# Column transform over 128 rows by moving turned chunks on chip, with fixed engine order and an earlier spectrum of the next image

## Chip, cores and metric

The kernel runs on one core of one Trainium2 chip. The metric is the device time of one execution in microseconds (us), the median of several runs. "PE" is TensorE, "DVE" VectorE, "ACT" ScalarE, "POOL" GpSimd and "SP" SyncE, which here does nothing but issue transfers.

## The reference, cut to what matters

The input is eight images of 8 channels, 256 by 256, in float32. After a group norm, four Fourier layers follow, then a two-layer head per pixel, and at the end a 3 by 3 dilation of the normed result.

```python
for i in range(4):
    h1 = _spectral_conv(h, sp_w1[i], sp_w2[i])   # rfft2, keep 12x12 low modes, mix channels, irfft2
    h2 = _gconv1x1(h, w_w[i], w_b[i])
    h = h1 + h2
    if i < 3:
        h = _gswish(h, betas[i])
h = _gswish(_gconv1x1(h, fc1_w, fc1_b), betas[3])   # head: 10 -> 128 per group
return _gconv1x1(h, fc2_w, fc2_b)                   #       128 -> 2 per group
```

The kernel does the transforms as matmuls with small cosine and sine tables. The *column transform* is the forward transform over the 256 columns (w), done for each chunk of 24 image rows as soon as the chunk has its new values. There are 11 chunks an image and layer, and layers 0, 1 and 2 need the column transform for the layer after them.

## The kernel before

PE is in program order (`manual_schedule(engines={PE})`); the other engines' order is left to the scheduler. A generator writes out the layers of image b and, after each `yield n`, some steps of the head of image b-1 (128 in all, in proportion to the counts n). `unit(main, late)` writes `main` now and the `late` part of the unit before it just after, so that a unit's dependent half comes one unit later.

```python
def turn(c):                                   # 32x32 blocks transposed by VectorE
    nc.vector.transpose(turned[:, c % 3], h[:, c].rearrange("p f w -> p (f w)"))
    ...                                        # returns the pair (c-1, c) when c is odd

def transform(chunks):                         # two chunks together, K = 32 rows
    ...
    for v in range(8):                         # 8 steps over the 256 columns
        for f in range(NQ):
            for q in range(NQ):
                mm(pair[q // 2][part(f), q % 2, :m], fw8[part(q), v, :],
                   t[part(q), :, f, :, v, : NBLK * WID], start=v == 0, stop=v == 7)
    ...                                        # copies to z, half on VectorE, half on ACT

def burst(c):                                  # a chunk of one layer
    ...                                        # 16 matmuls h2 (L461 or L458), 8 matmuls h1 (L464)
    nc.scalar.activation(dst, pair[i], AF.Silu)
    ...
    if l < 3:
        ready.append(turn(c))

for c in range(NCH):
    before = ready[c - 1] if l < 3 and c > 0 else None
    unit(partial(burst, c), partial(transform, before) if before is not None else None)
    yield 1
```

Between layers stand the row transform, the mixing by the spectral weights (`mix`, whose weights are loaded when they are needed) and the rebuilding of rows (`rows_of`); each has copies out of PSUM that alternate between VectorE and ACT. Each image begins with the spectrum of its own x.

Of the kernel before, what the change touches and what calls it, by code (L numbers as in the profile page):

```python
# [21 lines left out]
G = 4  # L22
# [17 lines left out]
STEPS = 128  # L40


@with_exitstack
def fno_dilate_kernel(ctx: ExitStack, tc: tile.TileContext, a: dict, out: bass.AP):
    nc = tc.nc
    mm = nc.tensor.matmul
    PE = mybir.EngineType.PE
# [25 lines left out]
    fw8 = load("fw8", (128, 8, 32))  # L73
# [8 lines left out]
    eh_q = load("eh_q", (128, 3, NBLK, 32))  # L82
# [7 lines left out]
    cz = load("cz", (32, 4, WID, G, 2))  # L90
# [9 lines left out]
    turned = const.tile([128, 3, 2048], F32, tag="turned", name="turned")  # L100
# [3 lines left out]
    for t in y_rows:  # L104
        for r in (0, C * HW + 1):
            nc.sync.dma_start(t[r : r + 1], yin[0:1, 0, :HW])
    fz = const.tile([128, WID, G, 32], F32, tag="fz", name="fz")
# [49 lines left out]
    for l in range(3):  # L157
        nc.vector.tensor_tensor(
            cz[0:1, l, :, :, 0], cz[0:1, l, :, :, 0],
            sp_a[0:1, 4 * l : 4 * l + 4].unsqueeze(1).to_broadcast([1, WID, G]), ALU.mult,  # L160
        )
    nc.vector.tensor_tensor(cz[0:1, 0, :, :, 0], cz[0:1, 0, :, :, 0], cv[0:1], ALU.add)
    nc.sync.dma_start(cz[25:26, 0, :, :, 0], cv[1:2])
    nc.sync.dma_start(cz[0:1, 0, :, :, 1], cv[2:3])
# [9 lines left out]
    def group_stats(chunks, name):  # L174
        n = len(chunks)
        st = sb.tile([128, n, 6], F32, tag="bn", name=f"bn_{name}")
        for i, c in enumerate(chunks):
            nc.vector.bn_stats(st[:, i, :], c)
        return stats_end(st, name)

    def stats_end(st, name):
        mv = sb.tile([128, 2], F32, tag="mv", name=f"mv_{name}")
        nc.vector.bn_aggr(mv, st.rearrange("p n s -> p (n s)"))
        p = ps_a(f"p_st_{name}")
        mm(p[:, 0:1], grp, mv[:, 0:1], start=True, stop=True)
        mr = sb.tile([128, 2], F32, tag="mr", bufs=4, name=f"mr_{name}")
        nc.vector.tensor_copy(mr[:, 0:1], p[:, 0:1])
        d = sb.tile([128, 1], F32, tag="d", name=f"d_{name}")
        nc.vector.tensor_tensor(d, mv[:, 0:1], mr[:, 0:1], ALU.subtract)
        nc.vector.scalar_tensor_tensor(mv[:, 1:2], d, d, mv[:, 1:2], ALU.mult, ALU.add)  # L190
        q = ps_a(f"p_sv_{name}")
        mm(q[:, 0:1], grp, mv[:, 1:2], start=True, stop=True)
        nc.vector.tensor_scalar(mr[:, 1:2], q[:, 0:1], EPS, None, ALU.add)
        nc.scalar.activation(mr[:, 1:2], mr[:, 1:2], AF.Sqrt)
        nc.vector.reciprocal(mr[:, 1:2], mr[:, 1:2])
        return mr
# [19 lines left out]
    def spectrum_x(b, out_):  # L216
# [6 lines left out]
        mr = group_stats([x[:, i // 4, 512 * (i % 4) : 512 * (i % 4 + 1)] for i in range(8)], f"x{b}")  # L223
        out_["mr"] = mr
        yield 1
        a0 = sb.tile([128, 128, 16], F32, tag="Z", bufs=1, name=f"a0_{b}")
        xt = turned[:, 2].rearrange("p (f r c) -> p f r c", f=2, r=8)
        for half in range(2):
            xn = x[:, half]
            nc.vector.tensor_scalar(xn, xn, mr[:, 0:1], mr[:, 1:2], ALU.subtract, ALU.mult)  # L230
            xn = xn.rearrange("p (r w) -> p r w", r=8)
            yield 1
            for r in range(0, 8, 4):
# [8 lines left out]
                nc.vector.tensor_copy(dst[:, 0], src[:, 0])  # L242
                nc.scalar.copy(dst[:, 1], src[:, 1])
# [11 lines left out]
        yield 1  # L255
# [39 lines left out]
    def spectrum_h(b, l, at, out_):  # L295

        rows = turned.rearrange("p t f -> p (t f)")[:, : NBLK * WID * 128]
        if l % 2 == 1:

            view = rows.rearrange("p (i g k) -> p i g k", g=G, k=32)  # L300
            for j0 in range(0, NBLK * WID, 8):
                n = min(8, NBLK * WID - j0)
                t = ps_z(f"p_at_{b}_{l}_{j0}")
                for i in range(n):
                    nc.tensor.transpose(
                        t[: CS * NQ, i // 4, 128 * (i % 4) : 128 * (i % 4 + 1)],
                        at[:, :CS, :, j0 + i].rearrange("p r j -> p (r j)"), ident)
                dst = rows[: CS * NQ, 128 * j0 : 128 * (j0 + n)]
                src = t[: CS * NQ].rearrange("p u w -> p (u w)")[:, : 128 * n]
                if (j0 // 8) % 2 == 0:  # L310
                    nc.vector.tensor_copy(dst, src)
                else:
                    nc.scalar.copy(dst, src)
                if j0 == 8:
                    yield 1
            eh, m = eh_f, CS * NQ
            yield 1
        else:

            view = rows.rearrange("p (g i k) -> p i g k", g=G, k=32)  # L320
            for g in range(G):
                nc.vector.transpose(
                    rows[:, 960 * g : 960 * (g + 1)].rearrange("p (i r) -> p i r", r=32),
                    at[:, :, g, : NBLK * WID].rearrange("p r i -> p i r"))
            eh, m = eh_q, 128
            yield 2
        p = ps_a(f"p_b_{b}_{l}")
        for k in range(2):
            for n in range(2 * NBLK):
                term, blk = n // NBLK, n % NBLK  # L330
                for q in range(4):
                    k0 = 12 * term + 3 * q
                    mm(p[part(q), 120 * k : 120 * k + 120], eh[:, spectrum_table(k, term), blk, :],
                       view[:m, WID * blk : WID * (blk + 1), :, k0 : k0 + 3],
# [13 lines left out]
    def mix(b, l, bt):  # L348

        s = [sb.tile([128, 3, G, 2, WID], F32, tag=f"S{i}", bufs=1, name=f"S{i}_{b}_{l}") for i in range(2)]  # L350
        for k in range(3):
            sw = sb.tile([128, G, 2 * WID, WID], F32, tag="sw", name=f"sw_{b}_{l}_{k}")
            nc.sync.dma_start(sw.rearrange("p g m i -> p (g m i)"), a["spw"][l, k])
            for k2 in range(2):
                pr = turned[:, 2, 1024 * k2 : 1024 * k2 + 800].rearrange("p (g m i) -> p g m i", g=G, i=WID)
                nc.vector.tensor_tensor(  # L356
                    pr, sw, bt[:, k2, k].unsqueeze(2).to_broadcast([128, G, 2 * WID, WID]), ALU.mult)
# [3 lines left out]
                )  # L361
        f = sb.tile([128, 2, 3, G, WID], F32, tag="F", bufs=1, name=f"F_{b}_{l}")
        nc.vector.tensor_tensor(f[:, 0], s[0][:, :, :, 0, :], s[1][:, :, :, 1, :], ALU.subtract)
        nc.vector.tensor_tensor(f[:, 1], s[0][:, :, :, 1, :], s[1][:, :, :, 0, :], ALU.add)
        yield 6
# [7 lines left out]
        nc.vector.tensor_copy(fz[0:32, :, :, 24:26], cz[:, l])  # L373
        for q in range(4):
            dst = fz[part(q), :, :, 6 * q : 6 * q + 6].rearrange("p o g k -> p k g o")
            src = p[part(q), :240].rearrange("p (k g o) -> p k g o", g=G, o=WID)
            if q % 2 == 0:
                nc.vector.tensor_copy(dst, src)
            else:
                nc.scalar.copy(dst, src)  # L380
        yield 1

    def rows_of(b, l, out_):

        z = sb.tile([128, 32, NQ, 32], F32, tag="Z", bufs=1, name=f"Z_{b}_{l}")
        nc.gpsimd.memset(z[:, :CS, :, NBLK * WID :], 0.0)
        nc.gpsimd.memset(z[:, CS:], 0.0)
        zv = z[:, :CS, :, : NBLK * WID].rearrange("p r f (n o) -> p o n r f", n=NBLK)
        for o in range(0, WID, 2):
# [10 lines left out]
            for u in range(2):  # L400
# [7 lines left out]
                if u == 0:  # L408
                    nc.vector.tensor_copy(dst, src)  # L409
                else:  # L410
                    nc.scalar.copy(dst, src)
            if o % 4 == 2:
                yield 1
        out_["z"] = z
        yield 1


    def layer(b, l, z, mr, stored):
        def turn(c):

            nc.vector.transpose(turned[:, c % 3], h[:, c].rearrange("p f w -> p (f w)"))  # L421
            if c % 2 == 1:
                return (c - 1, c)
            return (c,) if c == NCH - 1 else None

        def transform(chunks):

            done.append(chunks)
            order = sorted(chunks, key=lambda c: c % 3)
            n = len(order)  # L430
            lo = order[0] % 3
            step = order[-1] % 3 - lo if n == 2 else 1
            t = turned[:, lo : lo + step * (n - 1) + 1 : step].rearrange(
                "p n (f s v i) -> p n f s v i", f=NQ, s=2, v=8)
            m = 2 * n * NBLK * WID
            pair = [ps_z(f"p_d_{b}_{l}_{order[0]}_{i}") for i in range(2)]
            for v in range(8):
                for f in range(NQ):
                    for q in range(NQ):
                        mm(pair[q // 2][part(f), q % 2, :m], fw8[part(q), v, :],  # L440
                           t[part(q), :, f, :, v, : NBLK * WID], start=v == 0, stop=v == 7)
            for i in range(2):
                for k, c in enumerate(order):
                    dst = z[:, 2 * c : 2 * c + 2, 2 * i : 2 * i + 2, : NBLK * WID].rearrange("p s q i -> p q s i")
                    src = pair[i][:, :, 60 * k : 60 * k + 60].rearrange("p q (s i) -> p q s i", s=2)
                    if i == 0:
                        nc.vector.tensor_copy(dst, src)  # L447
                    else:
                        nc.scalar.copy(dst, src)  # L449
# [334 lines left out]
```

## Time and profile before

| | before |
|---|---|
| median of 4 fast runs (lowest, highest) | 5608.66 us (5593.67, 5617.1) |
| PE busy | 4647.9 us, 83% of the span |
| DVE, ACT busy | 2109.8 us (38%), 2860.7 us (51%) |
| bytes moved by DMA, packets | 354.52 MB, 74256 |
| mean granted clock of PE | 0.909 |

PE is the engine nearest to its limit, so what matters is which waits stand in front of PE's instructions. The view of waits has, for each engine and line, whom it waited for, the total in us, how many times, and the longest. These are four of the longest entries of PE:

```profile
PE p_d L440 <- issue: 215.4, 136, 4.3
PE p_g L393 <- ACT fz L380: 98.5, 16, 15.0
PE p_sv_x L192 <- DVE mv_x L190: 79.5, 8, 14.3
PE p_xt L236 <- ACT turned L243: 78.3, 13, 10.7
```

The second and the fourth say that PE stood still until ACT had finished a copy, the third that it stood for the statistics of x. They are what the smaller parts of the change go after. The forty slices, the groups and the timeline of this kernel are in the prediction.

### The profile page before, as it was taken

The page shows a single profiled execution, that of the slowest core. Times are in us where ns is not written, and L with a number is a line of the kernel's source. Part 1 is how long each engine was busy: PE and PEld are TensorE (multiplying, and loading weights), DVE is VectorE, ACT ScalarE, POOL GpSimd, SP SyncE. Part 2 cuts the span into 40 slices and gives each one's busy share as a digit, 9 for nine tenths or more (in the row PEclk, how much of TensorE's full clock was granted, in tenths as well). Part 3 has the DMA queues.
Part 4 walks back from the last instruction along what each step waited for, and adds up shares of the span by engine and source line. Part 5 has one row for each costly group of instructions (what it writes and reads, how often), then busy time and mean ns, then how long its engine had stood idle before and what let it go on. Part 6 is the DMA issues. An engine that isn't in the chain of part 4 may idle for free. (4 is left out here: it accounts for less than half of the span.)

```text
span 5622.9 us, 171099 instructions
## 1 busy us (share of the span) xinstructions
PE 4647.9 (83%) x80490; PEld 1907.3 (34%) x80490; DVE 2109.8 (38%) x2627; ACT 2860.7 (51%) x3269; POOL 280.2 (5%) x428
## 2 busy tenths in 40 slices
PE   5667899968998788887989779997799977999892
PEld 2433343323333233432434223342333423433220
DVE  5334333362333633245333442334433353332303
ACT  1223555545555445554555445554455544555682
POOL 1000000010000100000000000000000010000100
PEclk7779899979999799998999888998899988999996
DMA  2003100420014200041111411114101231102311
GB/s 62 11 11 143 36 34 30 148 81 23 32 41 156 69 34 29 26 162 64 34 41 47 141 56 37 34 60 140 50 30 34 97 118 36 34 30 102 101 61 49
DMA packets 74256, 354.52 MB, mean 63 GB/s; under 512 B 12691, under 2 KB 13967, under 8 KB 46863
## 3 DMA queue, kind: packets, MB, share of 16 engines
q0 software_dynamic: 37248, 176.18, 9.4%
q1 hardware_dynamic: 36303, 167.39, 8.7%
q8 instruction: 631, 10.34, 0.8%
q14 instruction: 74, 0.61, 0.0%
HBM read 217.70 MB, written 125.83 MB: 61 GB/s over the span
## 5 line engine op out<-in xcount | busy, mean ns | idle before, releaser
L529 ACT ACTIVATE act<-p_fc 128x1024 f32<-128x1024 f32 x2048 | 1981.7, 1022 | 627.1 <-PE p_fc L526 603.8
L526 PE MATMUL p_fc<-hs,c_w 32*128 32x512 f32 x8192 | 1458.8, 676 | 62.3 <-DVE o L584 29.1
L542 PE MATMUL p_fc<-act,c_w 128*32 128x512 f32 x8192 | 1177.0, 641 | 18.1 <-ACT act L529 13.5
L421 DVE STREAM_TRANSPOSE turned<-h 128x2048 f32<-128x2048 f32 x264 | 610.2, 2311 | 1082.2 <-ACT h L470 1082.2
L440 PE MATMUL p_d<-turned,c_fw 32*32 32x120 f32 (+1 forms) x36864 | 582.9, 275 | 346.5 <-issue 215.4
L470 ACT ACTIVATE h<-p_z 128x1024 f32<-128x1024 f32 x528 | 511.7, 1021 | 541.9 <-PE p_z L464 541.8
L526 PEld LDWEIGHTS p_fc<-hs,c_w 32*128 32x128 f32 x8192 | 485.0, 193 | 860.2 <-issue 360.4
L440 PEld LDWEIGHTS p_d<-turned,c_fw 32*32 32x32 f32 x36864 | 463.9, 106 | 539.8 <-issue 275.2
L461 PE MATMUL p_z<-h,c_wt 32*32 32x512 f32 x8448 | 517.3, 607 | 17.0 <-issue 9.4
L464 PE MATMUL p_z<-c_binv,Z 32*128 32x256 f32 x5632 | 439.6, 428 | 0.4 <-issue 0.4
L542 PEld LDWEIGHTS p_fc<-act,c_w 128*32 128x32 f32 x8192 | 167.9, 111 | 732.7 <-issue 672.8
L449 ACT COPY Z<-p_d 128x120 f32<-128x120 f32 x264 | 56.8, 263 | 681.6 <-PE p_d L440 681.6
L464 PEld LDWEIGHTS p_z<-c_binv,Z 32*128 32x128 f32 x5632 | 273.0, 197 | 323.9 <-issue 312.1
L447 DVE COPY Z<-p_d 128x120 f32<-128x120 f32 x264 | 63.5, 278 | 763.6 <-PE p_d L440 763.6
L472 DVE TENSOR_SCALAR h<-p_z,c_bias 128x1024 f32<-128x1024 f32 x88 | 112.9, 1283 | 359.5 <-PE p_z L464 359.5
L461 PEld LDWEIGHTS p_z<-h,c_wt 32*32 32x32 f32 x8448 | 96.2, 103 | 345.9 <-issue 107.9
L458 PE MATMUL p_z<-h,wc 6*32 6x512 f32 x2816 | 193.2, 668 | 8.2 <-issue 4.5
L409 DVE COPY Z<-p_g 128x264 f32<-128x264 f32 x160 | 98.0, 619 | 262.3 <-PE p_g L393 155.4
L393 PE MATMUL p_g<-c_rowg,fz 128*128 128x264 f32 x320 | 101.4, 466 | 98.5 <-ACT fz L380 98.5
L356 DVE TENSOR_TENSOR turned<-sw,B 128x800 f32<-128x800 f32 x192 | 180.5, 980 | 0.8 <-DMA sw<-in_spw 0.6
L358 DVE TENSOR_REDUCE S<-turned 128x80 f32<-128x800 f32 x192 | 179.4, 974 | 0.0
L546 DVE SCALAR_TENSOR_TENSOR y<-p_fc,c_b,y 128x512 f32<-128x512 f32 x64 | 47.9, 748 | 339.7 <-PE p_fc L542 339.7
(133 smaller groups left out, 2348.9 us busy)
## 6 DMA issues: line engine op xcount, KB each, us to landing
stored<-h SPq DMA_DIRECT2D x88, 1024.0 KB
hs<-stored POOLq DMA_DIRECT2D x88, 1024.0 KB, 5.1
sw<-in_spw SPq DMA_DIRECT2D x96, 400.0 KB
yin<-y_rows POOLq DMA_DIRECT2D x64, 512.0 KB, 4.8
h<-in_xp SPq DMA_DIRECT2D x352, 48.0 KB
turned<-in_x SPq DMA_DIRECT2D x16, 1024.0 KB
y<-in_x POOLq DMA_DIRECT2D x64, 256.0 KB, 3.0
y_rows<-y POOLq DMA_DIRECT2D x64, 256.0 KB, 2.3
```

Source lines behind the costliest of these rows:

```text
L356: nc.vector.tensor_tensor(pr, sw, bt[:, k2, k].unsqueeze(2).to_broadcast([128, G, 2 * WID, WID]), ALU.mult)
L358: nc.vector.tensor_reduce(s[k2][:, k].rearrange("p g s o -> p (g s o)"), pr.rearrange("p g m i -> p (g m) i"), AX.X, ALU.add,)
L421: nc.vector.transpose(turned[:, c % 3], h[:, c].rearrange("p f w -> p (f w)"))
L440: mm(pair[q // 2][part(f), q % 2, :m], fw8[part(q), v, :], t[part(q), :, f, :, v, : NBLK * WID], start=v == 0, stop=v == 7)
L458: mm(o, wc[k, :], h[k, c, f, :], start=True, stop=False)
L461: mm(o, wt[part(q), l, g, :], h[part(q), c, f, :], start=True, stop=False)
L464: mm(pair[q // 2][:, q % 2, HW * s : HW * (s + 1)], z[part(q), 2 * c + s].rearrange("p f o -> p (f o)"), binv[part(q), :], start=False, st ...
L470: nc.scalar.activation(dst, pair[i], AF.Silu)
L472: nc.vector.tensor_scalar(dst, pair[i], bias3, None, ALU.add)
L526: mm(pair[g // 2][:, g % 2, :], w1[part(g), blk, :], hs[c][part(g), j, :], start=True, stop=True)
L529: nc.scalar.activation(act[:, 2 * i : 2 * i + 2, :], pair[i], AF.Silu)
L542: mm(acc[part(g), :], w2[:, g, 15 - rb : 47 - rb], act[:, g, :], start=rb == 0, stop=rb == 15)
```

## The change

The intent has four parts. (1) The column transform shall contract 128 rows in two steps instead of 32 rows in eight; for that a turned chunk must lie the other way round over the partitions, so after the turn sixteen transfers move its blocks from one on-chip buffer to another. (2) VectorE and ACT get the program order too. (3) The spectrum of the next x and its first mixing stand beside the last layer of the image before. (4) The copies in the chains between layers go to VectorE, the weights of the mixing are loaded a layer earlier, and the chains get more places for head steps. A transform runs two chunks after its turn, which should hide the move.

```diff
-    with tc.manual_schedule(engines={PE}):
+    with tc.manual_schedule(engines={PE, DVE, ACT}):
...
-    turned = const.tile([128, 3, 2048], F32, tag="turned", name="turned")
+    turned = const.tile([128, 4, 2048], F32, tag="turned", name="turned")
...
         def turn(c):
+            k = c % 2
+            nc.vector.transpose(
+                turned[:, k].rearrange("p (v r i) -> p r v i", v=8, r=2 * NQ),
+                h[:, c].rearrange("p f (s v i) -> p (f s) v i", s=2, v=8))
+            src = turned[:, k].rearrange("p (v u x) -> p v u x", v=2, u=4)
+            dst = turned[:, 2 + k].rearrange("p (v q x) -> p v q x", v=2, q=NQ)
+            for q in range(NQ):
+                for u in range(4):
+                    nc.sync.dma_start(dst[part(u), :, q, :], src[part(q), :, u, :])
+
+        def transform(c):
+            t = turned[:, 2 + c % 2].rearrange("p (v q f s i) -> p v q f s i", v=2, q=NQ, f=NQ, s=2)
+            p = ps_a(f"p_d_{b}_{l}_{c}")
+            for v in range(2):
+                for g in range(G):
+                    m = t[:, v, g] if group_in_f else t[:, v, :, g]
+                    mm(p[part(g), :240], fw[:, v, :], m[:, :, :, : NBLK * WID], start=v == 0, stop=v == 1)
...
+        def after(c):
             if l < 3:
-                ready.append(turn(c))
+                turn(c)
+                if c > 1:
+                    transform(c - 2)
...
+            unit(partial(burst, c), partial(after, c))
+            next(side, None)          # a piece of the next x's spectrum, in layer 3
+            yield CHUNK               # CHUNK = 1.5
...                                   # zt replaces Z; fz, xt, at and row copies on VectorE;
...                                   # load_sw() a layer ahead; more yields in stats_end, mix, rows_of
```

## The prediction

> **What bounds the kernel now.** I read the forty slices first, then a table of three stretches, then the costliest groups, then two short pieces of the timeline. From the slices (busy tenths; PEclk is the granted TensorE clock):
>
> ```profile
> PE   5667899968998788887989779997799977999892
> PEclk7779899979999799998999888998899988999996
> DMA  2003100420014200041111411114101231102311
> ```
>
> TensorE is busy 80 to 90% of most slices, with seven dips. The first four slices are image 0, which has no head (fc1, silu, fc2) of an earlier image beside it; the dips that follow are the spectra of the next x. The table of stretches has length, then busy time of PE, weight loads, DVE, ACT, POOL, then granted clock, DMA share and GB/s:
>
> ```profile
> 216.00:254.00 38.00, 28.66 (x801) 14.91 (x792) 16.57 (x14) 15.24 (x19) 0.00 (x0) 0.90 0.01 3
> 511.00:5208.00 4697.00, 4041.68 (x70386) 1649.21 (x70388) 1776.03 (x2183) 2492.24 (x2849) 215.78 (x338) 0.93 0.19 63
> 5208.00:5623.00 415.00, 292.84 (x2086) 77.82 (x2080) 103.09 (x166) 256.13 (x265) 34.70 (x58) 0.86 0.21 69
> ```
>
> So the span is about 511 us for image 0, 4697/7 = 671 us for each of images 1 to 7, and 415 us of last head and dilation. In the middle PE is at 4042/4697 = 86% and the next engine, ACT, at 53%: PE's own stream of work sets the pace. The groups that the change touches:
>
> ```profile
> L440 PE MATMUL p_d<-turned,c_fw 32*32 32x120 f32 (+1 forms) x36864 | 582.9, 275 | 346.5 <-issue 215.4 <-ACT act L529 74.3 <-DVE turned L421 52.5
> L421 DVE STREAM_TRANSPOSE turned<-h 128x2048 f32<-128x2048 f32 x264 | 610.2, 2311 | 1082.2 <-ACT h L470 1082.2
> ```
>
> L440 is the column transform, 36864 small matmuls, 73 us of PE an image. The two pieces of timeline give the unit costs. First image 0 (start, length, engine, line, what, idle before it):
>
> ```profile
> 233.40 1.15 PE L464 MATMUL p_z<-c_binv,Z 32*128 32x256 f32 x16
> 234.58 1.94 ACT L470 ACTIVATE h<-p_z 128x1024 f32<-128x1024 f32 x2 [1.39 <-PE p_z L464]
> 236.55 2.31 DVE L421 STREAM_TRANSPOSE turned<-h 128x2048 f32<-128x2048 f32 x1 [1.01 <-ACT h L470]
> 238.92 4.55 PE L440 MATMUL p_d<-turned,c_fw 32*32 32x120 f32 x222 [4.37 <-DVE turned L421]
> ```
>
> This is the chain that decides my prediction: after a chunk's last matmul come two silus (1.94) and the turn (2.31), and PE, with nothing else to do, stood 4.37 us before the transform. Before the change that happens once for two chunks, in image 0 alone. With a head beside it:
>
> ```profile
> 818.86 1.07 PE L542 MATMUL p_fc<-act,c_w 128*32 128x512 f32 x8
> 819.85 1.16 PE L461 MATMUL p_z<-h,c_wt 32*32 32x512 f32 x32
> 820.94 1.15 PE L464 MATMUL p_z<-c_binv,Z 32*128 32x256 f32 x16
> ```
>
> A chunk's burst costs 2.2 us at full clock, one fc2 1.0, one fc1 about the same, so a head step 2.1.
>
> **What the skill says.** TensorE: Matmul & The Clock Gate, Part 1, says that PE runs at half clock after about 3.4 us of idleness and comes back after about as long busy. The trace agrees: in image 0, with its waits, slices are granted 0.7 to 0.9, in the middle mostly 0.9 and more. Part 3 of that page says that matmuls with 32 output columns overlap in different column groups; the trace has it in L542, eight instructions of about 640 ns each in 1.07 us. DMA: Bandwidth & Descriptors, Rules for kernel authors, says to coalesce many small transfers, as those under 64 KB pay mostly overhead. The trace shows the overhead as issue time on the SP queue, for loads on all partitions or on 32 (c_cz):
>
> ```profile
> 8.24 0.43 SPq L66 DMA_DIRECT2D c_wbd<-in_wbd  x1
> 8.72 0.43 SPq L66 DMA_DIRECT2D c_cz<-in_cz  x1
> 9.19 0.42 SPq L66 DMA_DIRECT2D c_wt<-in_wt  x1
> ```
>
> That is one per 0.47 us whatever the size. The landing record of a lone 1 KB transfer on this queue (issue at 21.96, landed at 23.24) adds about 1.2 us at the end.
>
> **The change part by part.**
>
> *Column transform.* 16 matmuls of 32 rows by 32 columns and 8 steps become 8 of 128 rows by 32 columns and 240 wide, 16 instructions a chunk. Counted by the L542 row, 16 x 240 = 3840 columns against 8 x 512 = 4096 in 1.07 us: 1.0 us a chunk instead of 73/33 = 2.2. Gain at most 33 x 1.2 = 40 us of PE an image, if it waits for nothing.
>
> *The move.* Each turn now ends with 16 transfers on SP of 64 KB, two runs of 1 KB on 32 partitions. Their bytes are little: a 1 KB packet takes 46 ns in the trace's packet records, 64 a DMA engine is 2.9 us. Their issue is not: 16 x 0.47 = 7.5 us for plain shapes. For two runs a partition I take 0.57 (my estimate: one third to one half of the 39% by which the POOL queue's two-level yin loads, 0.756 us, exceed its plain 0.545). So 16 x 0.57 + 1.2 = 10.3 us from the end of the turn to the last landing.
>
> *Is it hidden?* It looks as if two chunks hide it, since transform(c-2) follows turn(c). But turn(c) is called first, both use the buffer c mod 2, and the program order counts. In the built order the third turn's transfers (chunk 2) wait for no PE at all, and the first transform (chunk 0) waits on eight DMA semaphores for counts that only the transfers of chunk 2 reach. So the transform of c-2 reads what was just moved for c, and PE, which is in order, waits for the whole of turn(c): the intended lag is zero. (The values are then another chunk's rows. I put that error into a copy of the reference on the host and the output changed by 2e-6 at most, so it isn't caught by a comparison.) It holds for chunks 2 to 10 of three layers: 27 waits an image, 216 in all.
>
> *A waiting chunk.* From the end of the burst: 0.1 + 1.94 + 0.03 + 2.31 + 0.05 = 4.4, moves 10.3, transform 1.9 (half clock after such a wait), next burst 2.85 (the first half cold). That is 19.5 us. In the order of images 1 to 7, one fc2 and fc1 stand within the wait and cost nothing; 35 head steps of 128 fall into these 27 chunks, the 8 others stand outside: 8 x 2.3 / 27 = 0.7. So 20.2, and 27 x 20.2 = 545 us an image.
>
> *The rest of an image.* 93 head steps x 2.1 = 195; 17 chunks without the wait x 2.2 = 37; rows, inverse, mixing and x matmuls about 62 (by the rows of the costliest groups, a share of an eighth each, pipelined); 26 left for VectorE chains. 320 us. Here are the change's other parts: the x spectrum beside the last layer removes most of the dips, of which an image holds 671 x 14% = 94 us of idle PE; copies on VectorE instead of ACT cost nothing seen, as DVE is at 38%. I believe in a gain of some 30 to 50 us from these, and it is in the 320.
>
> *Image 0.* 85 us until the first burst as now, 27 x 19.5 = 527, 6 free chunks 20, transforms at the layer ends 9, three chains of about 40 us between layers (310 to 345 us is one now), 55 for the last layer, 50 for the rest of x and mixing beside nothing: about 870.
>
> *Sum.* 870 + 7 x (545 + 320) + 410 = 7335 us. I say 7350.
>
> **Rivals.** (1) The lag works as meant and the moves are hidden. The one-chunk delay of each transform call and the two extra buffers speak for it; the semaphore counts speak against. Then 671 - 40 - 45 = 586 an image, image 0 about 470, in all 470 + 7 x 586 + 410 = 4980, 11% faster. (2) The shape makes each issue dear: the only many-run SP transfer now, c_cz<-cv with 40 pieces, took 0.70 to 0.83 us. At 0.8 + 0.04 the moves take 14.6 instead of 10.3: 4.3 x 27 x 8 = 930 more, 8270. For it: that measurement; against: those are 4-byte pieces, and stored<-h with 128 pieces takes 0.35. (3) Moves issue at 0.38 (0.33 for a lone sw load, plus the gap): 7.3 us, 3 x 216 = 650 less, 6690. (4) VectorE becomes the bound through the fixed order: its 2110 us plus some 150 of copies is far below; I give it nothing.
>
> **Range and chances.** The issue interval, 0.38 to 0.84 us, spans 6690 to 8270 by itself and is what I know least; the clock after waits and the 320 add some 150 either way, partly cancelling. 6650 to 8250 holds 8 in 10. Even with moves of 7.3 us, a full clock and no leftover chain, an image needs 27 x 15.6 + 294 = 715 us, over the 671 of now, so the slower side has 0.95. I leave 0.03 for faster (the wait isn't what I read) and 0.02 for the same.
>
> **What would show it.** A p_d group of 4224 instructions with a long wait before it ended by DMA turned, some 12 us 216 times; SP busy with 4224 transfers at 0.4 to 0.6 us each in trains of sixteen; granted clock below 0.8 in the middle stretch; PE at some 55 to 65% of the span; image 0 near 870 us. Waits of p_d under 3 us, or a PE share above 85%, would prove the central step wrong. DMA intervals away from 0.57 would only shift the size.

## The result and the profile after

| | before | after |
|---|---|---|
| median of 4 fast runs | 5608.66 us | 8039.36 us |
| lowest to highest | 5593.67 to 5617.1 | 8034.96 to 8041.6 |
| ratio of fast runs | | 1.4337 (95% interval 1.43 to 1.4374) |
| PE busy | 4647.9 us (83%) | 4665.3 us (58%) |
| bytes by DMA, packets | 354.52 MB, 74256 | 627.58 MB, 411621 |
| mean granted clock | 0.909 | 0.751 |

A ratio here and below is the mean time of one kernel's fast runs over the mean of the other's in the same rounds, so it is not quite the ratio of the medians quoted. The kernel before was run again in each group of runs, with medians of 5607.62, 5620.09 and 5631.91 us.

The changed kernel is 43% slower, although PE's busy time is the same to half a per cent. That equality is a coincidence of two things: the page counts 48090 matmuls instead of 80490, and they run at a lower clock. In the run with two queues below, the same 48090 matmuls take 4114.7 us. The forty slices of the changed kernel:

```profile
PE   3444456393664845657556575556654566555795
...
PEclk6567677696776967778677786778776787767897
```

Most slices are only about half busy, and the granted clock is at 6 or 7 tenths in most of them. The three stretches (image 0 without a head beside it; images 1 to 7; the last head and dilation) say how much of it lies where:

```profile
0.00:810.00 810.00, 329.79 (x4140) 152.99 (x4140) 289.46 (x365) 85.06 (x89) 26.59 (x25) 0.65 0.30 81
810.00:7622.00 6812.00, 4017.96 (x41647) 1416.55 (x41646) 1927.07 (x2399) 2276.66 (x2342) 168.34 (x281) 0.76 0.27 78
7622.00:8037.00 415.00, 317.60 (x2309) 85.10 (x2304) 104.36 (x167) 277.44 (x288) 35.25 (x59) 0.88 0.21 72
```

A middle image now takes 6812/7 = 973 us, where it took 671. The two groups named in the prediction, and the issue of the transfers as the view of that one line shows it (shortest, median and longest in ns):

```profile
L421 PE MATMUL p_d<-turned,c_fw 128*32 128x240 f32 x4224 | 654.4, 566 | 2988.9 <-DMA turned<-turned 2988.9
...
L405 DVE STREAM_TRANSPOSE turned<-h 128x2048 f32<-128x2048 f32 x264 | 609.8, 2310 | 1070.3 <-ACT h L445 934.5
```

```profile
L412 SPq DMA_DIRECT2D turned<-turned x4224: 585/595/1651, 97.2 to 7499.4; - x192
```

PE stood 2988.9 us before the transforms, all of it ended by transfers between the turned buffers; over 216 waiting chunks that is 13.8 us each. (The view of waits counts 432 of them, as the transform of a chunk of layer 1 starts in four pieces, each behind its quarter of the train: 144 + 72 x 4.) SP needs 595 ns for one transfer. The chain that ended last, by line (the page gives PE's lines 41% of the span together):

```profile
SPq L412 27%; PE p_fc L522 10%; PE p_fc L538 9%; DMA turned<-turned 6%; DVE turned L405 5%; PE p_d L421 5%; PE p_z L439 5%; PE p_z L436 4%; ACT h L445 4%; PE p_z L433 1%; DVE S L346 1%; DVE turned L344 1%; PE p_b L317 1%; PE p_at L304 1%; DMA yin<-y_rows 1%
```

SP's queue holds 27% of the span, all on the one line of the move. The timeline of one chunk of image 2 shows the links (start, length, engine, line, what; idle before it in brackets):

```profile
1873.72 2.02 PE L433 MATMUL p_z<-h,wc 6*32 6x512 f32 x32
...
1875.67 2.10 PE L439 MATMUL p_z<-c_binv,zt 32*128 32x256 f32 x16
...
1877.80 1.94 ACT L445 ACTIVATE h<-p_z 128x1024 f32<-128x1024 f32 x2 [16.03 <-PE p_z L439]
...
1879.77 2.31 DVE L405 STREAM_TRANSPOSE turned<-h 128x2048 f32<-128x2048 f32 x1 [0.41 <-ACT h L445]
...
1894.21 1.82 PE L421 MATMUL p_d<-turned,c_fw 128*32 128x240 f32 x16 [13.15 <-DMA turned<-turned]
```

The first two lines are the burst. It starts at 1873.72, its silus at 1877.80 and the turn at 1879.77, which ends at 1882.08. The next transform starts at 1894.21. Within that gap the sixteen transfers of this turn are issued from 1882.16 to 1892.63, and the last lands some 1.6 us later. Nothing else that PE could do is allowed before it: the transform of chunk c-2 stands behind the whole move of chunk c.

### The profile page after: what moved, and what is told of

Same layout as the page of the kernel before. It is cut to its first block, busy times and chain, and to the rows that moved or that the text cites. A ratio compares the mean times of both kernels' runs of the same rounds, so it can differ in the third digit from the quotient of the medians.

```text
span 8039.8 us, 112626 instructions
## 1 busy us (share of the span) xinstructions
PE 4665.3 (58%) x48090; PEld 1654.6 (21%) x48090; DVE 2320.9 (29%) x2931; ACT 2639.2 (33%) x2717; POOL 230.2 (3%) x365
## 2 busy tenths in 40 slices
DMA packets 411621, 627.58 MB, mean 78 GB/s; under 512 B 80183, under 2 KB 351539, under 8 KB 384435
## 4 chain that ended last, share of the span: by engine, by line
PE 41%; SPq 27%; DVE 12%; DMA 7%; issue 7%; ACT 5%; POOL 0%; DVEq 0%; POOLq 0%; ACTq 0%
SPq L412 27%; PE p_fc L522 10%; PE p_fc L538 9%; DMA turned<-turned 6%; DVE turned L405 5%; PE p_d L421 5%; PE p_z L439 5%; PE p_z L436 4%; ACT h L445 4%; PE p_z L433 1%; DVE S L346 1%; DVE turned L344 1%; PE p_b L317 1%; PE p_at L304 1%; DMA yin<-y_rows 1%
## 5 line engine op out<-in xcount | busy, mean ns | idle before, releaser
L421 PE MATMUL p_d<-turned,c_fw 128*32 128x240 f32 x4224 | 654.4, 566 | 2988.9 <-DMA turned<-turned 2988.9
L522 PE MATMUL p_fc<-hs,c_w 32*128 32x512 f32 x8192 | 1406.5, 687 | 15.5 <-ACT act L525 9.4
L422 DVE COPY zt<-p_d 128x240 f32<-128x240 f32 x264 | 107.6, 407 | 3310.0 <-PE p_d L421 3310.0
L421 PEld LDWEIGHTS p_d<-turned,c_fw 128*32 128x32 f32 x4224 | 205.8, 147 | 3456.2 <-issue 3167.8
L439 PE MATMUL p_z<-c_binv,zt 32*128 32x256 f32 x5632 | 493.1, 470 | 0.1
L436 PE MATMUL p_z<-h,c_wt 32*32 32x512 f32 x8448 | 464.3, 744 | 23.4 <-ACT act L525 9.8
L439 PEld LDWEIGHTS p_z<-c_binv,zt 32*128 32x128 f32 x5632 | 309.3, 222 | 422.9 <-issue 404.1
L395 DVE COPY zt<-p_g 128x264 f32<-128x264 f32 x320 | 169.8, 610 | 208.4 <-PE p_g L380 106.0
L344 DVE TENSOR_TENSOR turned<-t,B 128x800 f32<-128x800 f32 x192 | 188.5, 982 | 3.8 <-DMA t<-in_spw 3.3
L449 ACT ACTIVATE h<-p_z,c_bias 128x1024 f32<-128x1024 f32 x88 | 98.1, 1115 | 210.3 <-PE p_z L439 210.3
```

Of the source, the lines that this page charges most:

```text
L344: nc.vector.tensor_tensor(pr, sw[k], bt[:, k2, k].unsqueeze(2).to_broadcast([128, G, 2 * WID, WID]), ALU.mult)
L421: mm(p[part(g), :240], fw[:, v, :], m[:, :, :, : NBLK * WID], start=v == 0, stop=v == 1)
L436: mm(o, wt[part(q), l, g, :], h[part(q), c, f, :], start=True, stop=False)
L439: mm(pair[q // 2][:, q % 2, HW * s : HW * (s + 1)], zt[part(q), 2 * c + s].rearrange("p f o -> p (f o)"), binv[part(q), :], start=False, s ...
L522: mm(pair[g // 2][:, g % 2, :], w1[part(g), blk, :], hs[c][part(g), j, :], start=True, stop=True)
```

## The experiments

### Swap the two calls (e1_swap)

```diff
         def after(c):
             if l < 3:
-                turn(c)
                 if c > 1:
                     transform(c - 2)
+                turn(c)
```

This is the smallest edit that gives the two chunks of lag. It also makes the transform read its own chunk, and not the one moved after it.

> Edit: after(c) calls transform(c-2) before turn(c), so that the lag of two chunks is real. Theory (the waits come from the order of the two calls, each wait is silu + turn + a train of 16 issues + landing): the wait before the column transform falls from some 13 us to under 5, and what is left is the SP queue, whose train of 16 x 0.64 = 10.2 us per chunk is longer than PE's own work of a chunk (2.2 + 1.0 + 1.3 x 2.1 = 6 us). The cycle falls from 22.5 to about 10.4 us, an image from 984 to about 650, and the whole to 5500 us (5300 to 5650), about the same as the kernel before. Rival (the moves are slow by latency or bandwidth whatever the order): cycles stay above 18 us and the time above 7000.

Measured over three rounds: 5722.09 us (5717.09 to 5725.32), ratio to before 1.0201 (1.0182 to 1.022). Of the 2317 us between the two medians of the changed kernel and this one, all came from two lines in another order. So the order of the calls is shown to be the main cause. But it did not reach the range that I gave. The groups and the chain say why:

```profile
L421 PE MATMUL p_d<-turned,c_fw 128*32 128x240 f32 x4224 | 494.1, 494 | 907.0 <-DMA turned<-turned 889.1
```

```profile
SPq L412 31%; PE p_fc L522 14%; PE p_fc L538 11%; DMA turned<-turned 7%; PE p_z L436 4%; PE p_z L439 4%; PE p_d L421 3%; PE p_at L304 1%; PE p_b L317 1%; DVE S L346 1%; PE p_g L380 1%; DVE turned L344 1%; PE p_g L385 1%; DMA yin<-y_rows 1%; PE p_a L250 1%
```

The wait of the transforms fell from 2988.9 to 907.0 us, not to nothing. The chain is now SP's: in images 1 to 7 a train starts every 11.0 us on average within a layer (10.6 to 11.4 in the middle half), which is the 16 transfers at an interval of 0.639 us (10.2 us) and a little. PE's own work for a chunk with its share of head steps is less, as the run with two queues below shows. So with the lag repaired, SP's issue sets the pace of the chunks.

### The change without the move (e2_old_transform)

```diff
         def turn(c):
-            ...sixteen transfers...
+            nc.vector.transpose(turned[:, c % 3], h[:, c].rearrange("p f w -> p (f w)"))
         def transform(chunks):
-            ...128 rows, 2 steps...
+            ...32 rows, 8 steps, two chunks together, as before...
```

The buffers and tables of the kernel before come back with it, and so does its row transform, which reads what the old column transform writes. All the other parts of the change stay.

> Edit: the changed kernel with the column transform of before put back (no moves; pairs of chunks, 32-row matmuls, the transposes it needs), all other parts of the change kept: fixed order on DVE and ACT, next x's spectrum beside the last layer, weights loaded earlier, chain copies on VectorE. Theory: these parts gain some 45 us for each of seven images, 5290 us (5200 to 5400), and the whole loss is the move. Rival (the fixed order or the copies on VectorE cost by themselves): 5608 or more.

Measured: 5300.3 us (5296.28 to 5303.42), ratio 0.9451 (0.9436 to 0.9466). This is the hit that it was expected to be. The busy tenths of PE:

```profile
PE   4666799998899988999898998999889998889992
```

The dips that the kernel before has seven times are mostly gone. The other parts of the change are worth 5.5%, and all of the loss comes from the move and the order around it.

### Half the transfers, and half the bytes (e3_half_count, e4_half_bytes)

Both are wrong on purpose: the transforms read rows that were set to zero at the start and are never moved (the outputs still passed the comparison, which does not see an error of this kind). Both keep the changed kernel's order of calls. The two buffers are zeroed first, because a read of rows that were never written would not be free of memory errors.

```diff
 e3
-                for u in range(4):
+                for u in range(2):
 e4
-                    nc.sync.dma_start(dst[part(u), :, q, :], src[part(q), :, u, :])
+                    nc.sync.dma_start(dst[part(u), 0, q, :], src[part(q), 0, u, :])
```

> Edit: 8 of the 16 transfers of each turn left out (half of the transfers and half of the bytes; wrong values on purpose). Theory (issue on SP is what the wait is made of): each of 216 waits is 8 x 0.64 = 5.1 us shorter, 8039 - 1106 = 6930 us (6800 to 7050). If latency of a transfer made the wait, the time would hardly move.

> Edit: all 16 transfers kept, but each moves one run of 1 KB per partition instead of two (half of the bytes; wrong values on purpose). If bytes set the length of the train, as long a gain as with half the count, 6930 us. If the issue costs a fixed time per transfer, 0.64 us stays and so does 8040. My theory lies between: 0.47 us as the plain loads of the kernel before have it, 16 x 0.17 x 216 = 590 us less, 7450 (7300 to 7600).

Each had one run, of unknown state. Half the count: 6716.64 us, a train of eight takes 5.07 us instead of 10.19, and a waiting chunk in images 1 to 7 takes 17.2 us on average instead of 22.5, about 5 less, as expected. The time is some 200 us lower than 216 chunks of 5.2 us less would make it, and below my range; the mean clock was 0.802 instead of 0.751, which fits, but I did not separate that. Half the bytes: 7928.81 us, which misses my range; the issue of a transfer with one run of 1 KB a partition instead of two:

```profile
L413 SPq DMA_DIRECT2D turned<-turned x4224: 507/589/1614, 101.0 to 7387.3; - x192
```

The median is 589 ns against 595, and the interval 0.633 us against 0.639. So the time of the wait goes with the number of transfers and hardly with their bytes. My prediction had taken the second run of each partition as the reason for a longer issue than that of plain loads (0.43 us); this run refutes that.

### Two issuing queues (e5_two_queues)

```diff
                 for u in range(4):
-                    nc.sync.dma_start(dst[part(u), :, q, :], src[part(q), :, u, :])
+                    queue = nc.sync if u % 2 == 0 else nc.gpsimd
+                    queue.dma_start(dst[part(u), :, q, :], src[part(q), :, u, :])
```

This is on top of the swap. The Trainium skill says, in DMA: Bandwidth & Descriptors, Issuing engines are not separate DMA queues, that issuing from several engines "will only save the time on the sequencer it takes to initiate the DMA, which is usually small relative to the DMA itself". If the issue is the bound, then just that time is what is wanted here.

> Edit: the swap of e1, and every second transfer of a train issued from the POOL queue instead of SP. Theory (in e1 SP's issue sets the chunk's cycle of 11 us): two trains of eight take 5.1 us each beside each other, the cycle falls to PE's own 6 to 7 us, an image from 672 to about 590 (e2's 631 less the 40 us that the wider transform saves), the whole to 5050 us (4950 to 5250). Rival (the DMA engines or the landing set the cycle): it stays near 11 us and the whole near 5700. A risk: POOL waits in order for its other loads and holds the moves up.

Measured: 4792.46 us (4786.34 to 4798.74), ratio 0.8528 (0.8505 to 0.8552), faster than the range that I gave. SP's half of a train takes 5.6 us instead of 10.8 for a whole one (medians), and a chunk of images 1 to 7 takes 7.3 us on average instead of 11. The slices of PE, then the issue of POOL's half:

```profile
PE   4665799998899979899899988999799988999991
```

```profile
L413 POOL DMA_DIRECT2D turned<-turned x2112: 539/539/1567, 97.9 to 4256.0; - x192
```

PE is busy for 8 or 9 tenths of most slices, and its mean clock is 0.928. POOL takes 539 ns for a transfer, about as long as SP, but the two issue side by side. (A run with all transfers on POOL was not made; at its interval of 0.53 us a train of sixteen would take 8.5 us, my estimate, so the faster issue of one engine alone does not give the 5.6.) The same 64 KB transfers, with the same bytes, cost the swapped kernel 930 us when one engine issued them. This kernel beats the kernel before by 14.7%, so the idea of the change was good and its loss lay in its execution.

### One train for two chunks (e6_pairs)

```diff
+            if k == 0 and c < NCH - 1:
+                return
-            src = turned[:, k].rearrange("p (v u x) -> p v u x", v=2, u=4)
-            dst = turned[:, 2 + k].rearrange("p (v q x) -> p v q x", v=2, q=NQ)
+            src = turned[:, 0 : k + 1].rearrange("p k (v u x) -> p (k v) u x", v=2, u=4)
+            dst = turned[:, 2 : k + 3].rearrange("p k (v q x) -> p (k v) q x", v=2, q=NQ)
```

Also on top of the swap, with the transforms called in pairs to match; it is the advice to coalesce, with 128 KB a transfer.

> Edit: the swap of e1, and one train of 16 for two chunks together (four runs of 1 KB per partition, 128 KB a transfer). Same bytes, half the transfers. Theory (a transfer's issue costs the same whatever it moves, as e4 showed for less): 10.2 us per two chunks on SP; the turn of the next even chunk must wait for the train to have read its buffer, so some 8 us a chunk instead of 11, 5130 us (5000 to 5350). If issue grew with the runs, 1 us each and no gain over e1's 5722.

Measured: 5905.45 us (5898.29 to 5911.85), ratio 1.051 (1.0477 to 1.0543), outside the range that I gave and slower than one train a chunk. The issue stayed as cheap as hoped: 601 ns for a transfer of twice the size, so SP's work was nearly halved. But VectorE's waits have an entry that the swapped kernel lacks (there it was 2.8 us):

```profile
DVE turned L405 <- DMA turned<-turned: 1191.4, 90, 17.9
```

A train for two chunks reads both source buffers, so the next turn waits until it has read them, and the transforms wait for the train. In one such cycle the transfers were under way to 1410, and only at 1410.26 did the next turn start, after 17.06 us of idleness. Pairing took away the second buffer on both sides of the move. The miss is mine: I had counted issues and not buffers.

### More head steps beside each chunk (e7_more_head)

```diff
-            yield CHUNK
+            yield 4 if l < 3 else CHUNK
```

On top of the swap; more of the 128 head steps then stand beside the moves, and fewer between layers.

> Edit: the swap of e1, and a chunk of layers 0 to 2 counts 4 instead of 1.5 in the sharing out of head steps, so that about 2.3 head steps instead of 1.3 stand in each of its cycles. Theory: the cycle stays at SP's 11 us and only fills up, and the head steps are missing later where they took time of their own: about 30 steps x 2.1 us x 7 images = 440 us less than e1, 5280 us (5100 to 5450).

Measured: 5584.34 us (5578.22 to 5587.05), ratio 0.9936 (0.991 to 0.9961), far less than expected. PE's two longest waits, first in the swapped kernel and then in this one:

```profile
PE p_d L421 <- DMA turned<-turned: 889.1, 304, 9.7
PE p_f L362 <- DVE F L354: 138.8, 18, 15.6
```

```profile
PE p_d L421 <- DMA turned<-turned: 703.3, 245, 9.5
PE p_f L362 <- DVE F L354: 228.4, 32, 15.6
```

The waits for transfers fell by 186 us only, and those for the mixing result F rose by 90. Head steps are a fixed supply: what covers the moves is missing in the chains between layers. And SP's pace remained: a train starts every 11.5 us on average.

### Where the other parts gain (e8_x_at_start, e9_copies_only, e10_fixed_order_only)

The first takes the kernel with the old transform and puts the spectrum of x back at the start of each image. The second is the kernel before with its copies in the chains on VectorE and nothing else changed. The third is the kernel before with one line changed.

```diff
 e8 (on e2)
+        yield from start(b, d)                       # at the start of each image
-            yield from layer(b, l, d, stored, then if l == 3 else iter(()))
+            yield from layer(b, l, d, stored, iter(()))
 e9 (on before, four places)
-                nc.scalar.copy(dst, src)
+                nc.vector.tensor_copy(dst, src)
 e10 (on before)
-    with tc.manual_schedule(engines={PE}):
+    with tc.manual_schedule(engines={PE, DVE, ACT}):
```

> Edit: e2 (old column transform) with the x spectrum and the first mixing put back to the start of each image; the fixed order and the copies on VectorE stay. Theory (the gain of e2 is that x's chain stands beside the last layer): it goes back to about 5550 us (5480 to 5650). Rival (the gain is the fixed order): it stays under 5400.

> The kernel before with one part of the change alone: four of its five kinds of ACT copies (x transpose, spectrum transpose, mixing result, row rebuild) moved to VectorE. Theory (of the part that the change gains, the copies are the largest): in the kernel before PE waits 98.5 + 14.6 us for ACT's copies of fz and 78.3 + 6.2 us for its copies of the x transpose, 198 us in all, because those copies queue behind silus; on VectorE some 45 us of such waits remain, as in the run with the old transform. So about 150 us less: 5460 (5400 to 5540). Rival (the fixed order of VectorE and ACT brings it): no more than 50 us less, above 5560.

> The kernel before with one line changed: VectorE and ACT in program order too, not only PE. Theory (copies): the ACT copies still stand behind silus, now without any freedom to move forward, so no gain: 5620 (5550 to 5750). Rival (the order itself): 5450 or less.

Measured: the x spectrum back at the start, 5390.92 us (ratio 0.9591, 0.9567 to 0.9616); the copies alone, 5629.03 us (1.0001, 0.9982 to 1.002); the order alone, 5514.1 us (0.9783, 0.9763 to 0.9802). I missed all three; for the first two the time lies where I had put the rival (under 5400, and above 5560). The place of the x spectrum is worth the step from 0.9591 to 0.9451, 1.4% of the kernel before, and not most of the 5.5%. The fixed order alone brings 2.2%, which I had given nothing. The copies alone bring nothing, although PE's waits for ACT's copies had come to nearly 200 us. PE's waits with the copies alone:

```profile
PE p_g L393 <- DVE fz L380: 114.7, 16, 18.7
...
PE p_xt L236 <- DVE turned L243: 34.3, 13, 4.5
PE p_a L248 <- DVE o L584: 31.5, 6, 6.0
```

The wait of p_g has only changed its releaser, from ACT's last copy of fz to VectorE's (98.5 to 114.7 us). That of p_xt fell, but a new one of 31.5 us came before p_a, behind the dilation's work on VectorE. At p_g PE stood for the chain, whoever made the copy; at p_xt a good part of what was won came back behind other work of VectorE. The view's PE waits add up to 893 us here and 872 us before. With the fixed order alone:

```profile
PE p_g L393 <- ACT fz L380: 121.6, 16, 19.0
...
PE p_st_x L185 <- DVE mv_x L183: 43.2, 8, 20.7
...
PE p_xt L236 <- ACT turned L243: 32.4, 6, 6.2
...
PE p_sv_x L192 <- DVE mv_x L190: 5.6, 8, 0.7
```

The wait of PE for the last statistics of x (p_sv_x, 79.5 us before) is down to 5.6 us, that for the first ones (p_st_x) went from 20.9 to 43.2, and p_xt behind ACT from 78.3 to 32.4. Two waits came that were small or absent before: p_xt behind VectorE (2.2 to 23.1 us) and p_f behind a step of the head on VectorE (41.4 us), while p_f behind F fell from 75.3 to 53.7. In total more went than came: the view's PE waits add up to 799 us with the fixed order. Why the order shortens the chains of x was not tested. The rest of the 5.5%, 1.9% between the order alone and the kernel with the x spectrum at its start, comes from the copies, the earlier weight loads and the added places for head steps together. These runs don't separate them.

### The better kernel with other counts (e11_two_queues_head2, e12_two_queues_head3)

```diff
-            yield CHUNK
+            yield 2.25 if l < 3 else CHUNK     # e11; 3 in e12
```

> The swapped kernel on two queues with the count of a chunk in layers 0 to 2 raised from 1.5 to 2.25, so that more head steps stand beside each chunk's move. In images 1 to 7 the transforms still wait 194 us for transfers. Theory: a step more in every third or fourth chunk takes about a third to a half of that away, while the wait for the mixing result (83 us) grows by some 20: 4730 (4690 to 4780). Rival (what is taken from the chains between layers is lost there in full): 4790 or more.

> The same with a count of 3. Theory: the chunks then wait hardly at all (some 50 us left) but the chains between layers have too few head steps, as the run with a count of 4 on one queue showed (its wait for the mixing result rose from 139 to 228 us): 4740 (4690 to 4810), no better than a count of 2.25. Rival (still SP's pace): under 4690.

Measured: 4783.28 us (4762.69 to 4791.65; ratio 0.8487, 0.8464 to 0.8511) with a count of 2.25, and 4850.17 us (0.8608, 0.8595 to 0.8622) with 3. The first does not differ clearly from the 0.8528 of the count 1.5, as its interval overlaps; the second is slower. With 2.25 the waits for transfers fell from 266.9 to 176.2 us and those for F rose from 137.6 to 171.1. With 3 they were 181.6 and 216.7. Both expectations were too hopeful about the waits for transfers. I leave the count as it was.

## Why the prediction was right, and where its terms were off

**The central step held.** "The transform of c-2 reads what was just moved for c, and PE, which is in order, waits for the whole of turn(c)". The trace has the wait, SP's queue is the largest single line of the chain, and the swap of the two calls took 2317 us away. The evidence named in the prediction came as told: waits of 13.8 us on average where I said some 12, a clock of 0.76 in the middle stretch where I said below 0.8, PE at 58% where I said 55 to 65%. Nothing in this central step was luck: it had been read from the program's order and semaphores, and the swap shows it.

**The sum was 9% low.** 8039 us lies inside the range, and 690 us above the middle. Term by term:

| term | predicted | measured |
|---|---|---|
| train of 16, first start to last end | 16 x 0.57 = 9.1 us | 10.19 us |
| last issue to transform | 1.2 us | 1.6 us (median) |
| burst after a wait, images 1 to 7 | 2.85 us | 3.2 us (mean; 2.2 to 4.1) |
| transform after a wait | 1.9 us | 1.82 us |
| cycle of a waiting chunk, images 1 to 7 | 20.2 us | 22.5 us |
| rest of a middle image | 320 us | 973 - 27 x 22.5 = 366 us |
| a middle image | 865 us | 973 us |
| image 0 | 870 us | 810 us |
| last head and dilation | 410 us | 415 us |

A waiting chunk has 4.4 us of silus and turn, the train, the landing, the transform and the burst, and what is left of 22.5 us, about 1 us, are the head steps outside the wait, where I had 0.7. The errors have the same sign in the chunks and in the rest of an image, and image 0 took 60 us back: in this the total was helped a little by chance.

*The issue interval* was the term that I called least known. I built 0.57 from the 0.47 of plain loads and an allowance for two runs a partition (the allowance as worded, a third to a half of 39%, gives only 0.53 to 0.56); it was 0.639. The half-bytes and the pairs runs show that neither runs nor bytes matter to it between 32 and 128 KB. It is a cost of the transfer itself, about 0.6 us on SP when it goes from on-chip memory to on-chip memory, on 32 partitions. What makes it longer than the 0.43 us of a load was not tested.

*The burst* I took as cold in its first half only. In the timeline of the changed kernel both its halves take nearly twice the 1.16 and 1.15 us that they take in the kernel before, and the fc2 matmuls after them took 1.94 us against 1.07. By the trace's clock records PE, which began the transform at 1871.97 and worked without a pause, was granted half clock until 1880.3, 8.4 us. But that chunk is not all of them: the next one had the full clock back after 3.2 us, and over the 126 waiting chunks of layers 0 and 2 in images 1 to 7 it took 2.9 to 9.8 us, in the median 5.2. (In layer 1 the transform starts in pieces, with waits between, so I leave it out.) The burst was 3.2 us on average, so this term was 0.4 us too small. I had followed the Trainium skill (TensorE: Matmul & The Clock Gate, Part 1), by which PE comes back after about 3.4 us of work. For most of these chunks that was too short, and the measurement decides.

*The rest of an image* was 46 us too low. In the middle stretch PE's idle time outside the transforms is 144 us, or 21 an image, near the 26 that I had set for it. So, by elimination, the excess is in the matmuls' own time, at a clock of 0.76 instead of 0.93. It is not split further.

*Image 0* went the other way. I took its cycle as 19.5 us with the silus and the burst on the path. The timeline of two chunks of image 0 in the changed kernel shows otherwise:

```profile
187.59 2.30 DVE L405 STREAM_TRANSPOSE turned<-h 128x2048 f32<-128x2048 f32 x1
...
190.01 1.94 ACT L445 ACTIVATE h<-p_z 128x1024 f32<-128x1024 f32 x2 [15.85 <-issue]
...
201.91 1.83 PE L421 MATMUL p_d<-turned,c_fw 128*32 128x240 f32 x16 [11.98 <-DMA turned<-turned]
...
205.37 2.30 DVE L405 STREAM_TRANSPOSE turned<-h 128x2048 f32<-128x2048 f32 x1
```

With no head step between, the unit after a burst is the next burst, so the turn of a chunk comes a whole burst later, and it starts at 187.59 before the silus of 190.01. The path is only turn, train, landing, transform and the copy and norm ahead of the next turn: 205.37 - 187.59 = 17.8 us. That is a chunk of layer 0; over the three layers the cycle was 16.1 to 18.2 us, on average 16.9. 27 x (19.5 - 16.9) is 70 us, a little more than the 60 that I had too much.

**The rivals.** The first, a lag that works, named 4980 us for it. The swap built that lag and took 5722: the number was wrong, since I asked only whether a move is hidden and not whether SP can issue one a chunk fast enough. It can't, at 10.2 us a chunk; with two queues the same lag gives 4792, below my number. The second, dear issues of 0.84 us, and the third, cheap ones of 0.38, are both refuted by 0.639. The fourth, VectorE as the bound, is refuted by its 29%.

**The smaller parts.** "I believe in a gain of some 30 to 50 us from these": the run with the old transform gained some 308 us in all (5.5% of 5608), 39 an image, so the size was right. The reason given was not: the x spectrum beside the last layer was to remove most of the dips, and it is worth about a quarter of the gain. The fixed order, to which I gave no gain, is worth more: 2.2%, measured on the kernel before.

## What to carry to other kernels

When a buffer is reused at a distance of two, the order of the two calls in the program decides whether the distance exists: a reader that is written after the next writer waits for that writer, and a comparison of outputs may not show it. A move made of many transfers has a rate as well as a latency: count issues times the interval on the issuing engine against the time between two moves, and if that is the bound, try to split the issues over a second queue before changing sizes: here the split took 930 us off, and the larger transfers cost a buffer and lost time. A wait's total in the profile is not the gain of removing its releaser; the next link of the same chain may end it just as late.

## What the Trainium skill lacked or had wrong

- DMA: Bandwidth & Descriptors, Issuing engines are not separate DMA queues, calls the time to initiate a DMA usually small relative to the DMA itself. For these 64 KB transfers from on-chip to on-chip memory it was the bound: 4224 of them at an interval of 0.639 us on SP. A second issuing engine took the swapped kernel from 5722 to 4792 us.
- The same page, Anatomy of one DMA, gives what one transfer costs, and not how often one engine can issue one. Here SP issued a transfer every 0.639 us and GpSimd every 0.53 (medians), and on SP 32, 64 and 128 KB took 589, 595 and 601 ns, so the size hardly mattered. A count of cycles for such an instruction stands elsewhere on the page, for "previous generations" and without a word whether this chip is among them.
- The same page, Rules for kernel authors, advises to coalesce small transfers. It does not say that this lengthens the hold on source and destination: with pairs of chunks the time rose from 5722 to 5905 us, with 1191 us of new waits of VectorE for the buffer.
- TensorE: Matmul & The Clock Gate, Part 1, has PE back at full clock after about 3.4 us of sustained work. Over 126 waiting chunks of the changed kernel it took 2.9 to 9.8 us from the start of the transform, in the median 5.2. The page says itself that its window runs free and the moment varies; the longest times here are well above its figure, and why was not tested.
